# An LSTM on one core: the weight sums of the first steps made earlier in fixed rooms, and the projection's work dealt anew over steps 6 to 15

## The chip, the cores and the metric

One core of a Trainium2 chip. The metric is the device time of one run in microseconds, the median of the runs measured: 3111.43 us for the kernel before (3110.64 to 3113.64 in 3 runs).

## The reference

An LSTM of 512 units over 512 time steps, batch 32, with the input added to its output:

```python
xW = jnp.einsum('ntd,dg->ntg', x, Wx) + b
def step(carry, xw_t):
    a = xw_t + prev_h @ Wh
    i, f, o = sigmoid(a[:, :H]), sigmoid(a[:, H:2*H]), sigmoid(a[:, 2*H:3*H])
    g = jnp.tanh(a[:, 3*H:])
    next_c = f * prev_c + i * g
    next_h = o * jnp.tanh(next_c)
out = x + hs
```

x is 32 x 512 x 512, Wx and Wh are 512 x 2048, all in float32. Each step needs the h of the step before it, so the 512 steps come one after the other. The projection x @ Wx doesn't depend on h and can be made at any time ahead of its step.

## The kernel before

**The step.** For each t, h_part (L239, its matmuls are L248) multiplies the last h by Wh: 16 matmuls of 128 rows by 512 columns, four column tiles by four parts of the contraction, into one PSUM bank that already holds the projection of that step. cell (L252) follows on ScalarE (ACT: sigmoids and tanh, L263 to L270) and VectorE (DVE: products, sum and transposition, L267 to L274). GpSimd (POOL) adds x (L282), and SyncE's queue (SP) stores the output two steps at a time (L286). While the cell runs, TensorE (PE) has nothing of the recurrence to do, so the projection of later steps is put there.

**The projection.** Steps 20 to 499 are projected in 20 groups of 24 steps. A group is done by a scheme that multiplies sums of blocks of x (U) with sums of blocks of the weights (V) and puts sums of the products (W) together; U_SUMS and U_OF (L48), V_SUMS and V_OF (L55), W_SUMS and W_OF (L62) name the terms. A group has 20 *slots*, a slot has seven products, and a product is an *item*: four matmuls of 256 columns each (L522), or 4 *units* of 64 columns. So a slot has 28 units and a group 560. The sequence of items over all slots is *the stream*; emit_matmuls sends so many units of it. Around it stand:

- u_op (L427) on DVE, which makes the sum of x-blocks that a slot needs, 128 x 896, in one of six rooms of ubuf; pair_sum (L483 to L489) on DVE, four operations of 128 x 768 per group, which the U sums read.
- load_v (L601) on SP, which loads the V sums of a row of the stream from DRAM (vdram) into the ring vring of three places, 128 x 1792 for a full row. A place is free when the items of its old row are done.
- seed_banks (L552) on ACT, which copies a bias row into the PSUM bank of a slot whose products start from one. There are five such banks, xbank; a sixth, bbank, holds one product of each slot, two slots at a time.
- evacuate, which takes finished products out of the banks: copies on ACT (L568, L577, L584), sums on DVE (L578, L581, L574) into rooms of cbuf. A bank is free for the slot after the next ones only when these are done.
- w_op (L392) on DVE, 128 x 1024, which makes sums of products; when an output block is complete, SP stores it to DRAM (L408), and load_xw (L613) brings it back, a step at a time, three steps ahead.

**The order.** It is written by hand: each engine does its instructions in the order in which the Python emits them, and waits for what it needs. w_op and evacuation are sent by a running balance of DVE's time (room["dve"]). From step 16 on every step has a like share of the stream, 23 and a third units on average.

**The head.** Steps 0 to 19 are projected plainly (plain_block, L181): per step 32 matmuls of 256 columns. The plain blocks of steps 0 to 4 and 7 come before step 0; HEAD_PLAINS says which are done beside the cell of which step, and keep (L774) adds the bias to them, in place (L776), into xw (L779), or into a parking place in cbuf (L783), whence SP stores it to kept (L784). From step 6 to 15 HEAD_STREAM gives the units of the stream of each step, 560 together, the first group. AHEAD_OF_CELL says how many units are emitted between h_part and the cell of a step (24 where it says nothing).

**The weight sums.** In the head the V sums are made too, on DVE: V_DIRECT are single blocks, V_FIRST and V_STEPS name the slots that are made before step 0 and beside steps 0 to 4. v_add (L672) does a sum in three operations (or one, of two made sums), in a room of vroom: three places of vring and three pairs of ubuf's rooms, which both are free until the stream starts. v_store (L684) then writes it to vdram, a large and a small DMA on SP. The bias rows of the seeds are loaded (load_seeds L735, load_raw_seeds L749), reworked on DVE (early_seeds L739 and L743, late_seeds L754 to L757) and four of the six copied by one DMA of SP from cbuf to r1 (move_seeds, L761). early_seeds stands after the V sums of step 4, pair_sum and the first U sums in step 5, late_seeds in step 6, and move_seeds after the last plain block's keep, in step 7.

jobs is a table from step to a list of such DVE work; it is shared out behind the plain blocks of the step (L908 to L912).

Of the kernel before, what the change touches and what calls it, by code (L numbers as in the profile page):

```python
# [37 lines left out]
LATE = (454, 456, 458, 460, 462, 470, 471)  # L38

FIRST = 7  # L40
HEAD_PLAINS = ((14, 15), (6, 16), (5, 17), (18, 19), (8, 11), (12,), (13,), (9, 10))
HEAD_STREAM = (0, 0, 0, 0, 0, 0, 32, 32, 56, 60, 60, 64, 64, 64, 64, 64)
AHEAD_OF_CELL = {7: 16, 8: 12}
V_DIRECT = (0, 2, 6, 9, 18, 19)
V_FIRST = (1,)
V_STEPS = ((3, 4, 5), (7, 8, 10), (11, 12, 13), (14, 15), (16, 17))

U_SUMS = {6: {3: 1, 5: -1}, 7: {1: 1, 6: 1}, 8: {2: 1, 3: -1}, 9: {2: 1, 7: -1}, 10: {0: 1, 1: -1}, 11: {0: 1, 4: -1}}  # L48
U_OF = [
# [5 lines left out]
V_SUMS = {8: {0: 1, 4: 1}, 9: {3: 1, 7: 1}, 10: {5: 1, 8: -1}, 11: {6: 1, 8: -1}, 12: {6: 1, 9: 1}, 13: {5: 1, 9: -1}}  # L55
V_OF = [
# [4 lines left out]
]  # L61
# [39 lines left out]
def kernel(  # L101
# [18 lines left out]
    xbank = [psum.tile([P, W], F32, name=f"xbank_{i}") for i in range(5)]  # L120
# [29 lines left out]
    def xslot(c):  # L150
        return 2 if c in (2, NCHUNK - 1) else c % 2

    def load_x(c, a=0, b=TC):
        nc.sync.dma_start(
            out=xnat[:, xslot(c), a:b].rearrange("p t q b -> p (t q b)"), in_=x[c][:, a * P : b * P]
        )
# [71 lines left out]
    def bank_of(t):  # L228
        if t < 9:
            g0, g1 = gbank  # L230
            return [g0, g1, xbank[3], xbank[4], xbank[0], g1, g0, xbank[3], xbank[4]][t]
        return gbank[t % 2]

    def half_of(t, i):
# [60 lines left out]

    free_c = [*range(6), 8, 9, 10, 6, 7]
    last_x = []
    free_u = list(range(6))  # L300
    room = {"dve": 0.0}

    def take(pool):
# [330 lines left out]
    vroom = [vring[:, i] for i in range(3)] + [  # L634
        ubuf[:, 2 * i : 2 * i + 2].rearrange("p a b c -> p (a b c)").rearrange("p (k c) -> p k c", k=7) for i in range(3)
    ]
    free_v = list(range(6))
    vt = {}
    v_uses = {}
    for terms in [*V_SUMS.values(), *V_OF]:  # L640
        for i in terms:
            v_uses[i] = v_uses.get(i, 0) + 1

    def tail_sums(a, b):

        z, w = r1[:, a:b], r2[:, a:b]
# [17 lines left out]
    def v_add(terms):  # L664
        (a, sa), (b, sb) = sorted(terms.items(), key=lambda v: -v[1])
        op = add if sb > 0 else sub
        dst = free_v.pop(0)
        if a > 7 and b > 7:
            op(flat(vroom[dst]), flat(vroom[vt[a]]), flat(vroom[vt[b]]))
        else:  # L670
            for d, pa, pb in zip(split_parts(vroom[dst]), v_parts(a), v_parts(b)):
                op(d, pa, pb)  # L672
        for i in (a, b):
            v_used(i)
        return dst

    def v_used(i):
        if i > 7:
            v_uses[i] -= 1
            if v_uses[i] == 0:  # L680
                free_v.append(vt[i])

    def v_store(s, parts, whole=None):
        dma = lambda o, i: nc.sync.dma_start(out=o, in_=i)  # L684
# [17 lines left out]
    def v_sum(i):  # L702
        if i > 7 and i not in vt:
            for k in V_SUMS[i]:
                v_sum(k)
            vt[i] = v_add(V_SUMS[i])

    def v_slot(s):

        terms = V_OF[s]  # L710
        for i in terms:
            v_sum(i)
        if len(terms) > 1:
            d = v_add(terms)
            v_stores.append(lambda: v_store(s, split_parts(vroom[d]), vroom[d]))
            free_v.append(d)
        else:
            (i,) = terms
            parts = v_parts(i)
            v_stores.append(lambda: v_store(s, parts, vroom[vt[i]] if i > 7 else None))  # L720
            v_used(i)

    v_stores = []

    def flush_v():
        for f in v_stores:
            f()
        v_stores.clear()
# [30 lines left out]
    def move_seeds():  # L759
        whole = lambda t: t.rearrange("p a s c -> p (a s c)")  # L760
        nc.sync.dma_start(out=whole(r1[:, 6:8]), in_=whole(cbuf[:, 6:8]))  # L761
# [12 lines left out]
    def keep(p):  # L774
        if p not in SEEDED:
            add(bank_of(p), bank_of(p), bias_full)  # L776
            return
        if p < PARKED:
            add(xw[:, p % 3], park_bank(p), bias_full)  # L779
            return  # L780
        n = p - PARKED
        dst = parks[n % 6]
        add(dst, park_bank(p), bias_full)  # L783
        kept_stores.append(lambda: nc.sync.dma_start(out=kept[n], in_=dst))  # L784

    with tc.manual_schedule():
# [40 lines left out]
        flush_v()  # L827
        for t in range(KEPT):
            add(bank_of(t), bank_of(t), bias_full)
        keep(FIRST)  # L830
        jobs = {}
        for t, ss in enumerate(V_STEPS):
            jobs.setdefault(t, []).extend([lambda s=s: v_slot(s) for s in ss])
        jobs[4].append(early_seeds)
        jobs[5] = [lambda i=i: pair_sum(0, i) for i in range(4)] + [lambda: u_ahead(28)]
        jobs[6] = [late_seeds]
        dve_jobs = []

        HEAD_STEPS = STREAM0
# [10 lines left out]
        for t in range(T):  # L850
# [15 lines left out]
            if last_x and t == last_x[0] + 3:  # L866
                load_x(NCHUNK - 1)
            assert last_x or t < SPLIT - 4
            if t == 3:
                load_x(2, 4, 8)  # L870
                load_seeds(((4, 3), (5, 1)), nc.sync)
                load_group(0)
            if t == 4:
                load_raw_seeds()
            if PARKED <= t + 3 < HEAD + NG * GS:
                load_xw(t + 3)
# [1 line left out]
            if t < HEAD_STEPS:  # L878
                plain = [("plain", p) for p in (HEAD_PLAINS[t] if t < len(HEAD_PLAINS) else ())]
                n_plain += len(plain)  # L880
                left = HEAD_STREAM[t]
                chunks = []
                if t >= len(HEAD_PLAINS) - 1:
                    chunks.append(("stream", AHEAD_OF_CELL.get(t, 24)))
                    left -= chunks[0][1]
                while plain or left:
                    if plain:
                        chunks.append(plain.pop(0))
                    m = min(left, 12)
                    if m:  # L890
                        chunks.append(("stream", m))
                        left -= m
                assert t < HEAD_STEPS - 1 or sum(HEAD_STREAM) == R * 7 * 4
                todo = jobs.pop(t, [])
                plains = sum(k == "plain" for k, _ in chunks)
                for i, (kind, m) in enumerate(chunks):
                    if kind == "plain":
                        bank = park_bank(m) if m in SEEDED else bank_of(m)
                        room["dve"] = 3000.0
                        for cc in range(4):  # L900
                            plain_block(m, cc, bank)
                        if i == 0:
                            cell(t)
                            if t + 1 in SEEDED:
                                seed_step(t + 1)
                        keep(m)
                        if m == HEAD_PLAINS[-1][-1]:
                            move_seeds()  # L908
                        last = i == plains - 1
                        for _ in range(len(todo) if last else -(-len(todo) // (plains - i))):  # L910
                            todo.pop(0)()
                            flush_v()  # L912
                    else:
                        load_v_ahead()
                        u_ahead(m)
                        if i == 0:
                            room["dve"] = min(room["dve"], 1000.0) + PLAIN
                        evacuate()
                        if t >= HEAD_STEPS - 3 and dve_jobs:
                            dve_jobs.pop(0)()  # L920
                        u_ahead(m + 24)
                        while wqueue and (room["dve"] > 800 or len(free_c) < 3):
                            w_op()
                        seed_banks(m)
                        emit_matmuls(m)
                        room["dve"] += m * PROD / 4
                        if i == 0:
                            cell(t)
                            room["dve"] -= 2500.0
                            if t + 1 in SEEDED:  # L930
                                seed_step(t + 1)
                if t >= 4:
                    load_v_ahead()
                if t == 10:
                    assert not v_stores
                    load_group(1)
                    group_loaded = 2
                    dve_jobs += [lambda i=i: pair_sum(1, i) for i in range(4)]
                continue
# [34 lines left out]
            while due and plain_tail:  # L974
                p, c, q = plain_tail[0]
                m = 2 if due > 1 and q % 2 == 0 else 1
# [6 lines left out]
            for p in kept_late:  # L983
# [3 lines left out]
                dst = late_halves.pop(0).rearrange("p s c -> p (s c)")  # L987
# [54 lines left out]
```

## Time and profile before

| what | value |
|---|---|
| median of 3 runs | 3111.43 us (3110.64 to 3113.64) |
| the profiled execution | 3112.65 us, span 3110.9 us |
| mean granted clock of TensorE | 0.999 |
| TensorE busy in the span | 3092.5 us (99%) |
| VectorE, ScalarE, GpSimd busy | 2229.6, 1451.8, 232.3 us |
| moved by the DMA queues | 761.44 MB, mean 245 GB/s |

How to read the lines that follow: a line of a timeline has the start in us from the span's start, the duration, the engine, the line of the kernel, the operation, what it writes and reads with the shape, the count of records put together in it, and in brackets the idle time of the engine before it with what ended that. TensorE's ends are modelled and reach a little into the next record. A matmul of float32 leaves two records. On SP a line is an issue of DMAs, not their transport. A line of the table by stretches has the stretch, its length, and the busy time (and count) of each engine in it, the granted clock, the busy share of the DMA engines and what they moved.

### The profile page before, as it was taken

To read this page: it belongs to the slowest core of one execution; us is meant where nothing else is said; L and a number is where in the kernel's file an instruction comes from. 1 tells how busy PE (TensorE), PEld (TensorE's weight loads), DVE (VectorE), ACT (ScalarE), POOL (GpSimd) and SP (SyncE) were. 2 spreads that over 40 slices of the span, in tenths; PEclk is the share of its full clock that TensorE was granted. 3 is DMA by queue.
4 is the path that set the end of the run, shared out by engine and by line. 5 is a ranking of instruction groups with operands and counts; after the bars stand their busy time and mean duration, and the time that the engine had idled before them with its cause. 6 is when DMAs were issued, how large, how long until landed. Compare 5 with 4: busy or idle time off the path is not lost.

```text
span 3110.9 us, 109178 instructions
## 1 busy us (share of the span) xinstructions
PE 3092.5 (99%) x44064; PEld 1674.5 (54%) x44064; DVE 2229.6 (72%) x6217; ACT 1451.8 (47%) x5484; POOL 232.3 (7%) x508
## 2 busy tenths in 40 slices
PE   9999999999999999999999999999999999999999
PEld 6644555555555555555555555555555555555576
DVE  6677776767676767777676767677776767677644
ACT  1344444444444444444444444444444444444444
POOL 0000000000000000000000000000000000000010
PEclk9999999999999999999999999999999999999999
DMA  9787878787777778787877777787877777778630
GB/s 334 281 265 264 265 245 258 233 267 241 256 253 249 255 243 267 245 263 236 259 244 255 253 249 254 248 258 248 270 230 256 246 254 251 256 250 276 198 92 21
DMA packets 307705, 761.44 MB, mean 245 GB/s; under 512 B 49024, under 2 KB 91776, under 8 KB 306560
## 3 DMA queue, kind: packets, MB, share of 16 engines
q1 hardware_dynamic: 307200, 754.45, 74.3%
q8 instruction: 348, 5.70, 0.8%
q14 instruction: 157, 1.29, 0.1%
HBM read 573.90 MB, written 179.31 MB: 242 GB/s over the span
## 4 chain that ended last, share of the span: by engine, by line
PE 93%; DVE 1%; ACT 0%; issue 0%; ACTq 0%; DVEq 0%
PE gbank L248 53%; PE xbank L522 32%; PE bbank L522 5%; PE xbank L248 2%; PE xbank L190 1%; DVE cbuf L392 0%; DVE prod L267 0%; DVE s L268 0%; ACT s L263 0%; DVE hbuf L272 0%; ACT tanh_c L270 0%; DVE ht L274 0%; DVE cbuf L578 0%; ACT cbuf L584 0%; DVE ubuf L427 0%
## 5 line engine op out<-in xcount | busy, mean ns | idle before, releaser
L248 PE MATMUL gbank<-wh_sb,ht 128*32 128x512 f32 (+1 forms) x16224 | 1778.2, 576 | 2.0 <-DVE ht L274 1.1
L248 PEld LDWEIGHTS gbank<-wh_sb,ht 128*32 128x32 f32 x16224 | 611.3, 110 | 823.3 <-issue 703.9
L522 PE MATMUL xbank<-vring,ubuf 128*32 128x256 f32 (+1 forms) x15464 | 957.5, 365 | 6.3 <-DMA vring<-vdram 3.6
L263 ACT ACTIVATE s<-gbank 128x128 f32<-128x128 f32 x976 | 274.1, 281 | 1277.5 <-PE gbank L248 1277.0
L522 PEld LDWEIGHTS xbank<-vring,ubuf 128*32 128x32 f32 x15464 | 591.5, 110 | 366.0 <-issue 189.9
L267 DVE TENSOR_TENSOR prod<-s 128x128 f32<-128x128 f32 x1024 | 293.7, 287 | 625.3 <-ACT s L264 625.2
L392 DVE TENSOR_TENSOR cbuf<-cbuf 128x1024 f32<-128x1024 f32 x408 | 490.3, 1215 | 1.5
L282 POOL TENSOR_TENSOR oc<-xnat,ht 128x128 f32<-128x128 f32 x504 | 232.1, 461 | 2839.8 <-DVE ht L274 1452.6
L270 ACT ACTIVATE tanh_c<-s 128x64 f32<-128x64 f32 x1024 | 262.4, 256 | 246.5 <-DVE s L268 244.4
L274 DVE STREAM_TRANSPOSE ht<-hbuf 128x64 f32<-128x64 f32 x1022 | 250.8, 245 | 76.2 <-DVE hbuf L272 3.2
L630 ACT COPY gbank<-xw 128x512 f32<-128x512 f32 x463 | 278.8, 602 | 0.1
L268 DVE TENSOR_TENSOR s<-prod 128x64 f32<-128x64 f32 x1024 | 230.5, 225 | 35.2
L568 ACT COPY cbuf<-xbank 128x512 f32<-128x512 f32 x374 | 218.5, 584 | 43.4 <-PE xbank L522 22.2
L272 DVE TENSOR_TENSOR hbuf<-o,tanh_c 128x64 f32<-128x64 f32 x1024 | 212.6, 208 | 28.2 <-ACT tanh_c L270 27.9
L264 ACT ACTIVATE s<-gbank 128x64 f32<-128x64 f32 x976 | 226.1, 232 | 0.0
L578 DVE TENSOR_TENSOR cbuf<-xbank,cbuf 128x256 f32<-128x256 f32 x374 | 153.2, 410 | 77.4 <-ACT cbuf L577 74.6
L522 PE MATMUL bbank<-vring,ubuf 128*32 128x256 f32 (+1 forms) x2704 | 200.6, 355 | 1.9 <-DVE cbuf L574 1.9
L522 PE MATMUL xbank<-vring,xs 128*32 128x256 f32 (+1 forms) x2472 | 174.6, 374 | 1.6 <-ACT xbank L552 0.9
L522 PE MATMUL xbank<-vring,r 128*32 128x256 f32 (+1 forms) x2480 | 173.3, 372 | 0.0
L265 ACT ACTIVATE o<-gbank 128x128 f32<-128x128 f32 (+1 forms) x507 | 155.2, 306 | 0.0
L581 DVE TENSOR_TENSOR cbuf<-xbank,cbuf 128x256 f32<-128x256 f32 x374 | 151.9, 406 | 0.0
L574 DVE TENSOR_TENSOR cbuf<-bbank,cbuf 128x256 f32<-128x256 f32 x374 | 151.4, 405 | 0.0
(104 smaller groups left out, 1803.7 us busy)
## 6 DMA issues: line engine op xcount, KB each, us to landing
vring<-vdram SPq DMA_DIRECT2D x340, 896.0 KB, 5.6
xw<-xwd SPq DMA_DIRECT2D x1920, 64.0 KB, 4.5
xwd<-cbuf SPq DMA_DIRECT2D x221, 512.0 KB, 4.5
out_dram<-oc SPq DMA_DIRECT2D x255, 128.0 KB, 3.7
xnat<-in_x_dram SPq DMA_DIRECT2D x62, 512.0 KB, 5.3
xs<-in_x_grouped_dram SPq DMA_DIRECT2D x10, 1536.0 KB, 8.7
vring<-vdram SPq DMA_DIRECT2D x20, 768.0 KB, 6.6
r<-in_x_grouped_dram SPq DMA_DIRECT2D x10, 1536.0 KB, 8.8
```

What stands on the lines that cost most here:

```text
L248: nc.tensor.matmul(dst[j * B : (j + 1) * B], state["ht"][:, k], m, start=False, stop=True, skip_group_check=True)
L263: nc.scalar.activation(s[:, u, 0:2], g[:, n_, 0:2], AF.Sigmoid)
L264: nc.scalar.activation(s[:, u, 2], g[:, n_, 3], AF.Tanh)
L267: nc.vector.tensor_mul(prod[:, u], s[:, u, 0:2], s[:, u, 2:4])
L268: add(nxt[:, u, 3], prod[:, u, 0], prod[:, u, 1])
L270: nc.scalar.activation(tanh_c[:, HALVES[u]], nxt[:, u, 3], AF.Tanh)
L274: nc.vector.transpose(ht[:, 2 * u : 2 * u + 2].rearrange("p q b -> p (q b)"), hbuf[:, HALVES[u]])
L282: (nc.gpsimd if t < T - 8 else nc.vector).tensor_add(oc[:, tt % 2], x_of(t), ht)
L392: op(c_of(dst), c_of(src), c_of(bb))
L522: nc.tensor.matmul(dst[j * B : (j + 1) * B, cols], left_of(gr, s, r)[:, j * B : (j + 1) * B], vring[:, row % 3, RIGHT[r], cols], start=sta ...
L568: nc.scalar.copy(t[:, 0:4:3], xb.rearrange("p (n c) -> p n c", n=2))
L630: nc.scalar.copy(bank_of(t), src)
```

## The change

- **Rooms.** The list of free rooms of the V sums (free_v, v_uses, v_used) goes. V_ROOMS says for each sum in turn which of the six rooms it is put in; rooms 0 to 2 are vring's.
- **Times of the V sums.** Slot 3 (V_NEXT) is made among the bias adds before step 0, V_SUMS[8] in step 1, and V_STEPS has four entries in place of five, so the last slots, 15 to 17, are made in step 3. early_seeds stays in step 4, without V sums ahead of it.
- **Loads.** The second half of x's chunk 2 is loaded in step 9 (was step 3), the three raw bias rows in step 6 (was step 4).
- **Bias rows.** late_seeds and move_seeds go to step 8, behind its plain block; two rooms of cbuf (6 and 7), which these rows occupy, come into the list of free rooms then.
- **Plain blocks.** Block 10 stays in step 7 and block 9 goes to step 8 (both were in step 7); step 7's bank is gbank[1] (was xbank[3]). What is in jobs is shared out evenly behind the plain blocks.
- **Stream.** Steps 6 to 15 have 36, 36, 60, 60, 60, 60, 64, 60, 64, 60 units (were 32, 32, 56, 60, 60, 64, 64, 64, 64, 64), 560 as before. Ahead of the cell are 24 units in step 7 (were 16) and 4 in step 8 (were 12).
- **Second group.** Its x is loaded from step 8 (was 10) and its pair sums are made from step 10 (were from 13). load_v_ahead is called from step 3 at a step's end (was 4). ubuf's rooms are taken in the order 2, 3, 4, 5, 0, 1.

```diff
-HEAD_PLAINS = ((14, 15), (6, 16), (5, 17), (18, 19), (8, 11), (12,), (13,), (9, 10))
-HEAD_STREAM = (0, 0, 0, 0, 0, 0, 32, 32, 56, 60, 60, 64, 64, 64, 64, 64)
-AHEAD_OF_CELL = {7: 16, 8: 12}
+HEAD_PLAINS = ((14, 15), (6, 16), (5, 17), (18, 19), (8, 11), (12,), (13,), (10,), (9,))
+HEAD_STREAM = (0, 0, 0, 0, 0, 0, 36, 36, 60, 60, 60, 60, 64, 60, 64, 60)
+AHEAD_OF_CELL = {8: 4}
...
-V_STEPS = ((3, 4, 5), (7, 8, 10), (11, 12, 13), (14, 15), (16, 17))
+V_NEXT = (3,)
+V_STEPS = ((4, 5, 7), (8, 10), (11, 12, 13, 14), (15, 16, 17))
+V_ROOMS = (0, 1, 2, 3, 4, 5, 2, 1, 3, 0, 4, 5, 3, 2)
...
-            return [g0, g1, xbank[3], xbank[4], xbank[0], g1, g0, xbank[3], xbank[4]][t]
+            return [g0, g1, xbank[3], xbank[4], xbank[0], g1, g0, g1, xbank[4]][t]
...
-    free_c = [*range(6), 8, 9, 10, 6, 7]
+    free_c = [*range(6), 8, 9, 10]
-    free_u = list(range(6))
+    free_u = [2, 3, 4, 5, 0, 1]
...
-    free_v = list(range(6))
+    rooms = list(V_ROOMS)
...
-        dst = free_v.pop(0)
+        dst = rooms.pop(0)
...
         for t in range(KEPT):
             add(bank_of(t), bank_of(t), bias_full)
+            if t == 1:
+                for s in V_NEXT:
+                    v_slot(s)
+                flush_v()
...
-        jobs[4].append(early_seeds)
+        jobs[1].append(lambda: v_sum(8))
+        jobs[4] = [early_seeds]
         jobs[5] = [lambda i=i: pair_sum(0, i) for i in range(4)] + [lambda: u_ahead(28)]
-        jobs[6] = [late_seeds]
+        jobs[8] = [late_seeds, move_seeds, lambda: free_c.extend((6, 7))]
...
+            if t == 9:
+                load_x(2, 4, 8)
             if t == 3:
-                load_x(2, 4, 8)
                 load_seeds(((4, 3), (5, 1)), nc.sync)
                 load_group(0)
-            if t == 4:
+            if t == 6:
                 load_raw_seeds()
...
-                if t >= len(HEAD_PLAINS) - 1:
+                if t > 6:
                     chunks.append(("stream", AHEAD_OF_CELL.get(t, 24)))
...
-                        if m == HEAD_PLAINS[-1][-1]:
-                            move_seeds()
-                        last = i == plains - 1
-                        for _ in range(len(todo) if last else -(-len(todo) // (plains - i))):
+                        plains -= 1
+                        for _ in range(-(-len(todo) // (plains + 1))):
...
-                        if t >= HEAD_STEPS - 3 and dve_jobs:
+                        if t >= 10 and dve_jobs:
...
-                if t >= 4:
+                if t >= 3:
                     load_v_ahead()
-                if t == 10:
+                if t == 8:
                     load_group(1)
```

More of the change, by code (lines that the diff above doesn't have):

```diff
@@ L636 @@
     ]
-    free_v = list(range(6))
+    rooms = list(V_ROOMS)
     vt = {}
[L639 to L642, printed above, removed]
     def tail_sums(a, b):
@@ L672, in v_add @@
                 op(d, pa, pb)
-        for i in (a, b):
-            v_used(i)
-        return dst
[L677 to L681, printed above, removed]
+        return dst
     def v_store(s, parts, whole=None):
@@ L715, in v_slot @@
             v_stores.append(lambda: v_store(s, split_parts(vroom[d]), vroom[d]))
-            free_v.append(d)
         else:
@@ L720, in v_slot @@
             v_stores.append(lambda: v_store(s, parts, vroom[vt[i]] if i > 7 else None))
-            v_used(i)
     v_stores = []
```

## The prediction, made before the changed kernel was run

> **What bounds the kernel now.** I read the page first (sums, then the chain), then the table by stretches, then TensorE's timeline up to 210 us, and last the timelines of VectorE (DVE), ScalarE (ACT) and the DMA queue (SP) around TensorE's waits. The page:
>
> ```profile
> span 3110.9 us, 109178 instructions
> PE 3092.5 (99%) x44064; PEld 1674.5 (54%) x44064; DVE 2229.6 (72%) x6217; ACT 1451.8 (47%) x5484; POOL 232.3 (7%) x508
> PE 93%; DVE 1%; ACT 0%; issue 0%; ACTq 0%; DVEq 0%
> ```
>
> TensorE is busy 3092.5 of 3110.9 us, so only 18.4 us of the span can be won without taking matmuls away, and the order of matmuls in both kernels counts the same number. The table by stretches says where the 18.4 us lie:
>
> ```profile
> core 0: us, PE busy (x) PEld busy (x) DVE busy (x) ACT busy (x) POOL busy (x), PEclk, DMA share, GB/s
> 95.40:98.81 3.41, 1.39 (x24) 0.50 (x16) 3.17 (x13) 2.01 (x5) 0.46 (x1) 1.00 0.87 281
> 98.81:102.23 3.42, 3.20 (x32) 1.58 (x32) 1.98 (x3) 0.74 (x2) 0.00 (x0) 0.50 0.92 284
> 300.00:2900.00 2600.00, 2599.89 (x36100) 1370.10 (x36094) 1911.63 (x5332) 1258.84 (x4697) 200.62 (x437) 1.00 0.78 252
> ```
>
> From 300 to 2900 us 0.11 us are idle, and the change does not touch what follows. What it can move is the head, and there are eight waits of TensorE in it:
>
> ```profile
> 97.25 1.07 PE L522 MATMUL xbank<-vring,ubuf 128*32 128x256 f32 x16 [1.54 <-DMA vring<-vdram]
> 99.03 1.94 PE L522 MATMUL xbank<-vring,xs 128*32 128x256 f32 x16 [0.71 <-ACT cbuf L568]
> 103.78 1.07 PE L522 MATMUL xbank<-vring,ubuf 128*32 128x256 f32 x16 [1.26 <-DMA vring<-vdram]
> 155.77 1.07 PE L522 MATMUL xbank<-vring,xs 128*32 128x256 f32 x16 [0.90 <-ACT xbank L552]
> 159.76 0.64 PE L522 MATMUL xbank<-vring,ubuf 128*32 128x256 f32 x8 [0.77 <-DMA vring<-vdram]
> 167.71 1.93 PE L522 MATMUL xbank<-vring,ubuf 128*32 128x256 f32 x32 [1.28 <-ACT xbank L552]
> 180.56 0.64 PE L522 MATMUL xbank<-vring,ubuf 128*32 128x256 f32 x8 [1.45 <-DVE cbuf L578]
> 195.80 0.64 PE L522 MATMUL bbank<-vring,ubuf 128*32 128x256 f32 x8 [1.87 <-DVE cbuf L574]
> ```
>
> Their sum is 9.78 us. To it comes the clock: 98.81 to 102.23 ran at 0.50, so 3.42 us did 1.7 us of work. The head's losses are 9.8 + 1.7 = **11.5 us, the most that the change can win** (0.37%). A measurement of this kernel tells about 0.2%, 6.2 us, from no change.
>
> **The change, part by part.** Durations are rows of this execution (3112.65 us, span 3110.9, so 1.75 us lie around the span); I compare losses of the head and put the difference on the median, 3111.43, which is 1.2 us lower. Where something stands in the changed kernel comes from the two kernels' orders of instructions: I let each instruction begin when the one before it on its engine and the one it waits for are over. Laid out so, the old order gives 6.9 us for the waits on DVE and ACT whose rows sum to 5.5 (leaving out the first three and the DMA's 0.77), about a third of a microsecond too much each; I take that off below. Units first:
>
> ```profile
> 104.64 3.64 PE L248 MATMUL xbank<-wh_sb,ht 128*32 128x512 f32 x32
> 108.07 1.07 PE L522 MATMUL xbank<-vring,xs 128*32 128x256 f32 x16
> 109.80 3.71 PE L181 MATMUL gbank<-r,xnat 128*32 128x256 f32 x64
> 113.55 0.70 DVE L776 TENSOR_TENSOR gbank<-gbank,bias_full 128x512 f32<-128x512 f32 x1 [2.91 <-PE gbank L181]
> 114.16 0.41 DVE L578 TENSOR_TENSOR cbuf<-xbank,cbuf 128x256 f32<-128x256 f32 x1
> 115.15 1.08 DVE L427 TENSOR_TENSOR ubuf<-xs 128x896 f32<-128x896 f32 x1
> ```
>
> A recurrent part takes 108.07 - 104.64 = 3.43 us. Two items of the stream (8 units) lie between 103.78 and 104.64, so an item is 0.43 us. A plain block begun at 109.80 leaves TensorE free at 113.23 (64 records at the 0.054 us that follows from an item's 8 records in 0.43), and its bias add starts 0.32 us later. On DVE the add holds the engine 0.61 us (to the next start), and so on for each row.
>
> *Weight sums a step earlier, x and bias rows moved behind them.* In before the last weight sum is over at 83.3; in the changed order it stands in step 3, and the adds ahead of it end at about 75.6, 7.7 us earlier. Its stores are issued earlier, and the first three row loads with them:
>
> ```profile
> 85.12 3.71 SPq L684 DMA_DIRECT2D vdram<-vring x4
> 94.56 1.28 SPq L601 DMA_DIRECT2D vring<-vdram x3
> 118.29 0.53 SPq L761 DMA_DIRECT2D r<-cbuf x1
> 145.79 0.55 SPq L474 DMA_DIRECT2D r<-in_x_grouped_dram x1
> ```
>
> ```profile
> 82.08 1.28 DVE L672 TENSOR_TENSOR vring<-cbuf,vring 128x768 f32<-128x768 f32 x2
> ```
>
> ```profile
> DMA packets 3014, 5.15 MB, mean 368 GB/s; under 512 B 204, under 2 KB 826, under 8 KB 3011
> ```
>
> The second is the DMA view of 80 to 94 us: the engines moved 368 GB/s, near the 400 of the best stretch below, so of the 7.7 us only about 5 arrive: I put the first rows at 92 to 96 us instead of 97 to 104. The 1.54 and 1.26 us go. **What is late next** stands at the same place, on DVE and ACT:
>
> ```profile
> 88.87 0.69 DVE L779 TENSOR_TENSOR xw<-bbank,bias_full 128x512 f32<-128x512 f32 x1 [1.14 <-PE bbank L181]
> 89.48 0.95 DVE L483 TENSOR_TENSOR xs<-xs 128x768 f32<-128x768 f32 x1
> 95.21 0.28 DVE L267 TENSOR_TENSOR prod<-s 128x128 f32<-128x128 f32 x1
> 97.08 0.69 DVE L779 TENSOR_TENSOR xw<-xbank,bias_full 128x512 f32<-128x512 f32 x1
> 97.69 1.08 DVE L754 TENSOR_TENSOR cbuf<-cbuf 128x256 f32<-128x256 f32 x3
> 100.14 0.69 DVE L757 TENSOR_TENSOR cbuf<-cbuf 128x512 f32<-128x512 f32 x1
> 97.80 0.59 ACT L552 COPY xbank<-seeds_own 128x512 f32<-128x512 f32 x1 [0.76 <-DVE xw L779]
> ```
>
> The third item needs its bank seeded (L552), the seed needs the bank that the add at 97.08 reads, and that add stands behind 8.2 us of DVE work without a gap, begun by a plain block's end (the bracket at 88.87). None of it is moved. The seed is done at 98.39 in both. The idle time before 97.25 begins at 95.71, where the plain block's last matmul ends by the model; the next could begin some 0.25 earlier, at 95.45. With its rows there TensorE does two items (0.86) and waits from 96.3 to 98.4: **2.1 us** (was 1.54 + 0.71, with the 1.26 behind).
>
> *Bias rows' sums (late_seeds) from step 6 to step 8.* 97.69 to 100.83 is 3.1 us of DVE that lay beside TensorE's waits. At step 8 they stand behind plain block 9 and ahead of a U sum that the stream needs. DVE from TensorE's leaving the block: 0.32 + 0.61 (bias add) + 3.1 + 1.08 (L427) = 5.1 us. TensorE has seven items, 3.0 us: **2.1 us of wait**. If the sums were absent, 2.0 against 3.0, it would be 0: this is the edit's whole price.
>
> *Plain block 10 at step 7 with stream behind it.* DVE: 0.32 + 0.61 + 0.41 (L578) = 1.35 us to the release of the bank that the second item needs; one item is cover: **0.9 us**. In before a second plain block hid this.
>
> *Pair sums of group 1 from step 13 to step 10; steps 10 to 12 dealt 60, 60, 64.* Two sums of 0.87 us (a row like L483, to the next start) now come between evacuations and U sums. By the order three waits of 0.95, 0.45 and 1.3 us, less 0.4 for the bias of the layout: **2.3 us** (bounds 1 and 4; was 0.90 + 1.28).
>
> *Steps 13 and 15.* Before:
>
> ```profile
> 171.12 5.06 DVE L392 TENSOR_TENSOR cbuf<-cbuf 128x1024 f32<-128x1024 f32 x4
> 191.25 0.42 DVE L578 TENSOR_TENSOR cbuf<-xbank,cbuf 128x256 f32<-128x256 f32 x1 [0.68 <-ACT cbuf L577]
> 191.59 3.48 DVE L392 TENSOR_TENSOR cbuf<-cbuf 128x1024 f32<-128x1024 f32 x3
> 195.33 0.41 DVE L574 TENSOR_TENSOR cbuf<-bbank,cbuf 128x256 f32<-128x256 f32 x1
> ```
>
> At step 15 the chain from L578 to L574's end, 4.5 us, left 1.87 us of wait, so six items were beside it. The new deal leaves the same chain with four items: 1.87 + 2 x 0.43 = 2.7; I take **2.5**. At step 13 four output sums (5.06), two evacuations (0.7), a U sum (1.0), a cell (1.9, as from 95.21 to 97.08 above) and L574 (0.4) make 9.0 us ahead of a bank; a recurrent part and six items (6.0 us) cover it: 3.0, less the layout's third twice (DVE and ACT both stand in the chain), **2.4** (was 1.45). Bounds for both: 1.4 and 3.2 each.
>
> *DMA behind the moved loads.* No row shows the new order of the queue; I bound it by the two rates that the head's queue had:
>
> ```profile
> DMA packets 1103, 2.66 MB, mean 266 GB/s; under 512 B 116, under 2 KB 262, under 8 KB 1103
> DMA packets 730, 2.00 MB, mean 400 GB/s; under 512 B 85, under 2 KB 93, under 8 KB 729
> ```
>
> (94 to 104 us and 103 to 108 us. Sizes are those of the tiles: a full row 0.92 MB, a kept or bias row 0.26.) The fourth row load now has ahead of it the third row, two outputs, six kept stores and three bias rows: with it 4.3 MB from about 91 us, landing at 102 by the one rate and 107.3 by the other, and some latency behind; TensorE wants it at 106. From 0 to 3 us, I take 1.0. The seventh row stands behind move_seeds, which waits on SP for late_seeds (about 125 us): 0 to 0.6, I take 0.4. Then move_seeds (1.05 MB), three rows, group 1's x (1.57), half a chunk of x and an output block go ahead of the tenth, with it 7.1 MB from 125 us, landing at 143 to 152 where it is wanted at 146.5: 0 to 5, I take 1.5. Together **2.9 us** (0 to 8.6; was 0.77 and 1.26).
>
> *Clock.* The row of 95.40 to 98.81 holds 2.02 us of idle, and the next stretch of the same length ran at half; the 1.87 us at 195.80 was followed by full clock. The changed kernel has five waits of 2 us or a little more. How they fall is chance; I take one halved stretch, **1.7 us** (0 to 5).
>
> [...]
>
> Costed at nothing: rooms from a table (no instruction of its own); two weight sums moved up among the bias adds (the banks behind them are read by the cells of steps 2 to 4, with TensorE at plain blocks meanwhile; without that cover some 2 us each, a 0.95 and two 0.6 steps as at 82.08); the half chunk of x at step 9 (first read by POOL at step 20; without that time 256 KB, under 1 us at the rates below).
>
> **Sum** of the head's losses after: 2.1 + 2.1 + 0.9 + 2.3 + 2.5 + 2.4 + 2.9 + 1.7 = 16.9, against 11.5: **+5.4 us, 3116.8, called 3117**.
>
> **The rivals.**
> 1. *The loads come in a burst and the clock trips again and again.* For it: 7.1 MB behind one wait of SP, five waits near 2 us. Against: the queue had 400 GB/s when it was full. It decides from 300 GB/s down: 12.3 of engine waits + 6 of DMA + 3.4 to 5 of clock = 22.5, **3122.5**, slower than before by 0.35%.
> 2. *Rows in time, no half clock*: DVE's waits alone, 12.3 against 11.5, **3112**: no difference; the wait on DMA is replaced by one on DVE, exactly.
> 3. *The clock does not halve, DMA as forecast*: 15.2, **3115**.
> 4. *DVE is not the bound after step 9* (the other side): the waits at steps 13 and 15 are one backlog, which the lighter deal (60 for 64) drains; then rows in time and full clock leave 2.1 + 2.1 + 0.9 + 1 = 6.1 us against 11.5: **3106**. It decides where the output sums come in ones and twos, not in fours; the order of instructions has them in fours and threes, which speaks against it.
>
> **How the numbers follow.** Forecast (3115.5 to 3119) 0.39; rival 1 (3119 to 3125) 0.22; rival 2 (3110 to 3113) 0.14; rival 3 (3113 to 3115.5) 0.13; rival 4 (3102 to 3109) 0.12. Range for 8 in 10: 3108.5 to 3122.5; it leaves out most of rival 4 and the upper part of rival 1. Slower by over 0.2% is above 3117.65: rival 1 and four tenths of the forecast, 0.38. Faster is below 3105.2: half of rival 4, 0.06. Within: 0.56. The first three that lie within 0.2% differ in what the traces show, not in a verdict.
>
> **What would show it.** Right: the first wait of the stream named ACT L552 and 2 us long; a wait of about 2 us at step 8 on a U sum (L427's successor), with late_seeds ahead of it on DVE; L574 as releaser of the two last waits; DMA waits at the fourth and tenth row. Wrong: a first wait under 1 us, no wait at step 8, or any change of the stretch from 300 to 2900 us, which I hold equal.

## The result and the profile after

The changed kernel took 3119.07 us (median of 12 runs, 3116.80 to 3121.97), the kernel before 3112.23 in the 12 runs beside them (3110.55 to 3114.35): a ratio of 1.0022, 95% interval 1.0013 to 1.0031, or 6.8 us slower. The forecast was 5.4 slower (3116.8, called 3117). The profiled execution of the changed kernel took 3121.97 us, 2.9 more than its median; of before's, 3112.65. Line numbers differ: up to the weight sums they are higher by two (L524 is L522 of before, L554 is L552), behind them lower by thirteen (late_seeds is L741 to L744, move_seeds L748, the bias adds L763 and L766).

The page's sums and the table by stretches, after:

```profile
span 3120.1 us, 109177 instructions
PE 3097.1 (99%) x44064; PEld 1674.1 (54%) x44064; DVE 2232.1 (72%) x6217; ACT 1452.7 (47%) x5484; POOL 233.1 (7%) x508
```

```profile
300.00:2900.00 2600.00, 2599.79 (x36072) 1369.97 (x36068) 1913.84 (x5325) 1258.25 (x4690) 201.18 (x437) 1.00 0.78 252
```

From 300 to 2900 us nothing changed, 0.21 us idle against 0.11. All of it is in the head. TensorE's timeline after, its waits up to 210 us:

```profile
98.56 1.07 PE L524 MATMUL xbank<-vring,xs 128*32 128x256 f32 x16 [1.88 <-ACT xbank L554]
107.42 1.07 PE L524 MATMUL xbank<-vring,xs 128*32 128x256 f32 x16 [0.91 <-DMA vring<-vdram]
113.55 0.64 PE L524 MATMUL xbank<-vring,xs 128*32 128x256 f32 x8 [0.69 <-DVE cbuf L580]
127.14 1.93 PE L524 MATMUL xbank<-vring,ubuf 128*32 128x256 f32 x32 [1.88 <-issue]
136.52 4.05 PE L524 MATMUL xbank<-vring,ubuf 128*32 128x256 f32 x40 [2.71 <-DMA vring<-vdram]
154.46 1.07 PE L524 MATMUL xbank<-vring,ubuf 128*32 128x256 f32 x16 [0.53 <-ACT cbuf L586]
163.01 0.64 PE L524 MATMUL xbank<-vring,ubuf 128*32 128x256 f32 x8 [0.16 <-DVE cbuf L580]
165.91 1.07 PE L524 MATMUL xbank<-vring,ubuf 128*32 128x256 f32 x16 [1.17 <-ACT cbuf L586]
186.70 0.64 PE L524 MATMUL bbank<-vring,ubuf 128*32 128x256 f32 x8 [2.42 <-DVE cbuf L576]
203.40 0.64 PE L524 MATMUL bbank<-vring,ubuf 128*32 128x256 f32 x8 [2.31 <-DVE cbuf L576]
```

Their sum is 14.66 us, against 9.78 before. The two DMA waits ahead of 104 us are gone; the seed's wait is in their place (98.56), and four waits of about 2 us or more are new or larger. The clock adds to it. Stretches of 3.41 us of the changed kernel (length, busy time by engine, then the granted clock as the third number from the end), each wait followed by the stretch behind it:

```profile
133.17:136.58 3.41, 0.69 (x12) 0.10 (x8) 1.69 (x8) 1.36 (x7) 0.26 (x1) 1.00 1.01 415
136.58:140.00 3.42, 3.42 (x36) 2.12 (x40) 0.00 (x0) 0.59 (x1) 0.20 (x1) 0.50 1.01 401
184.37:187.79 3.42, 1.09 (x20) 0.68 (x24) 2.53 (x12) 2.06 (x6) 0.46 (x1) 1.00 1.00 288
187.79:191.20 3.41, 3.41 (x36) 1.74 (x32) 1.75 (x3) 1.07 (x3) 0.00 (x0) 0.50 0.98 380
201.44:204.86 3.42, 1.46 (x24) 0.76 (x28) 3.42 (x6) 0.32 (x1) 0.00 (x0) 1.00 0.26 99
204.86:208.27 3.41, 3.41 (x22) 1.08 (x16) 2.62 (x4) 0.05 (x1) 0.00 (x0) 0.50 1.01 253
95.62:99.03 3.41, 1.53 (x31) 0.85 (x26) 2.08 (x8) 2.10 (x5) 0.45 (x1) 1.00 1.03 392
99.03:102.44 3.41, 3.41 (x60) 1.81 (x56) 1.42 (x2) 1.98 (x4) 0.00 (x0) 1.00 0.63 204
```

Three stretches ran at 0.50 behind 2.72, 2.33 and 1.96 us of idle; behind 1.88 the clock stayed at 1.00. Three halved stretches are 3 x 1.7 = 5.1 us of work lost; before had one. Waits and clock make 14.66 + 5.1 = 19.8 us after and 11.5 before: 8.3 of the 9.3 us between the two profiled executions. The same sum, taken from the profiled execution's time, leaves 3100.2 to 3102.2 us in these two kernels and in every kernel below, so it accounts for each of them within about 1 us.

### The profile page after: what moved, and what is told of

Read it like the earlier page. It is cut to its first block, busy times and chain, and to the rows that moved or that the text cites. A ratio compares the mean times of both kernels' runs of the same rounds, so it can differ in the third digit from the quotient of the medians.

```text
span 3120.1 us, 109177 instructions
## 1 busy us (share of the span) xinstructions
PE 3097.1 (99%) x44064; PEld 1674.1 (54%) x44064; DVE 2232.1 (72%) x6217; ACT 1452.7 (47%) x5484; POOL 233.1 (7%) x508
## 4 chain that ended last, share of the span: by engine, by line
PE 97%; DVE 1%; DMA 1%; ACT 0%; SPq 0%; issue 0%; DVEq 0%; ACTq 0%
PE gbank L250 53%; PE xbank L524 33%; PE bbank L524 5%; PE xbank L250 2%; PE xbank L192 1%; PE xbank L183 1%; PE gbank L183 1%; DMA vring<-vdram 1%; DMA vdram<-vring 0%; DVE cbuf L394 0%; PE xbank L798 0%; PE bbank L183 0%; DVE prod L269 0%; DVE s L270 0%; SPq L771 0%
## 5 line engine op out<-in xcount | busy, mean ns | idle before, releaser
L524 PE MATMUL xbank<-vring,ubuf 128*32 128x256 f32 (+1 forms) x15464 | 961.1, 365 | 6.5 <-DMA vring<-vdram 2.7
L524 PEld LDWEIGHTS xbank<-vring,ubuf 128*32 128x32 f32 x15464 | 595.2, 110 | 365.4 <-issue 193.7
L524 PE MATMUL bbank<-vring,ubuf 128*32 128x256 f32 (+1 forms) x2704 | 200.8, 355 | 4.8 <-DVE cbuf L576 4.7
L524 PE MATMUL xbank<-vring,xs 128*32 128x256 f32 (+1 forms) x2472 | 174.1, 373 | 3.5 <-ACT xbank L554 1.9
L524 PE MATMUL xbank<-vring,r 128*32 128x256 f32 (+1 forms) x2480 | 173.8, 372 | 0.0
L576 DVE TENSOR_TENSOR cbuf<-bbank,cbuf 128x256 f32<-128x256 f32 x374 | 151.6, 405 | 0.1
```

The lines of the kernel that those rows point to most:

```text
L524: nc.tensor.matmul(dst[j * B : (j + 1) * B, cols], left_of(gr, s, r)[:, j * B : (j + 1) * B], vring[:, row % 3, RIGHT[r], cols], start=sta ...
```

## The experiments

All were timed in five rounds beside the kernel before; differences are to the median of before in the runs beside them (3113.10 in the first four, 3112.86 in the next four, 3112.46 in the last two). The intervals reach about 2.8 us to each side, so smaller differences between two experiments rest on their traces. The theory was that each part has its own price, set by the order on an engine; the rival, that the loads come in a burst and the DMA queue is the limit.

**1. The bias sums back in step 6.**

```diff
-            if t == 6:
+            if t == 4:
                 load_raw_seeds()
...
-        jobs[8] = [late_seeds, move_seeds, lambda: free_c.extend((6, 7))]
+        jobs[6] = [late_seeds]
+        jobs[8] = [move_seeds, lambda: free_c.extend((6, 7))]
```

> The changed kernel with the raw bias rows loaded in step 4 and their sums made in step 6 again, as before the change; move_seeds stays in step 8, all else as changed. Theory (the engines' orders): the 1.88 us wait at step 8 goes, because DVE has 3.1 us less ahead of the U sum; SP is no longer held until 126 us by move_seeds, so the seventh row load is issued some 3 us earlier and its 2.71 us wait shrinks to under 0.5; with it at least one halved stretch (1.7 us) goes. 4.5 to 6.5 us less than the changed kernel, 3113 to 3114.5. Rival (the burst of loads on the DMA queue): the loads still come together, the wait at the seventh or tenth row stays at 2 us or more, and only the 1.9 us go: 3117.

Measured 3113.53 us, +0.4 (ratio 0.9994 to 1.0012), where the changed kernel stood at +6.8. Both waits, at step 8 and at the seventh row, are gone, and with them one halved stretch (two were left). The wait of 0.91 us at the fourth row is gone, too: the raw bias rows are loaded in step 4 again, so the price of this part holds the moved load as well as the moved sums. The mechanism in the changed kernel, DVE's timeline:

```profile
122.28 0.70 DVE L763 TENSOR_TENSOR gbank<-gbank,bias_full 128x512 f32<-128x512 f32 x1 [1.61 <-PE gbank L183]
122.89 1.09 DVE L741 TENSOR_TENSOR cbuf<-cbuf 128x256 f32<-128x256 f32 x3
125.35 0.69 DVE L744 TENSOR_TENSOR cbuf<-cbuf 128x512 f32<-128x512 f32 x1
125.95 1.09 DVE L429 TENSOR_TENSOR ubuf<-xs 128x896 f32<-128x896 f32 x1
```

The U sum that TensorE needs begins when the bias sums end; it ends at 127.04, and the matmul that the timeline gives to "issue" begins at 127.14.

**2. The seventh row's load ahead of move_seeds.**

```diff
-        jobs[8] = [late_seeds, move_seeds, lambda: free_c.extend((6, 7))]
+        jobs[8] = [late_seeds, load_v_ahead, move_seeds, lambda: free_c.extend((6, 7))]
```

> The changed kernel with one call moved: the seventh row load is emitted ahead of move_seeds in step 8, so that it isn't held behind SP's wait for the bias rows' sums; all else as changed. Theory (SP's order): the load is issued at about 122 us, when its place in the ring is free, instead of 126.7; the 2.71 us wait goes and the halved stretch behind it with it; the wait at step 8 (1.9) stays. 2.7 to 4.4 us less than the changed kernel: 3114.7 to 3116.4. Rival (the queue's rate is the limit): the eighth or the tenth row is late in its place by 2 us or more, and the time stays within 1 us of the changed kernel's, 3118 to 3120.

Measured 3116.63 us, +3.5 (1.0002 to 1.0019): 3.3 less than the changed kernel, in the theory's range by the difference. SP's queue, changed kernel and experiment:

```profile
126.11 0.53 SPq L748 DMA_DIRECT2D r<-cbuf  x1
126.69 4.05 SPq L603 DMA_DIRECT2D vring<-vdram  x3
```

```profile
117.91 0.32 SPq L603 DMA_DIRECT2D vring<-vdram  x1
125.23 0.53 SPq L748 DMA_DIRECT2D r<-cbuf  x1
125.86 4.01 SPq L603 DMA_DIRECT2D vring<-vdram  x2
```

The load could have gone at 118 us; SP waited 8 us for the bias sums ahead of it. The rest of the burst is the same, and behind it only one wait of 0.29 us on a row was left (at the fourth row's place, ahead of it, 0.63 us stayed, which the timeline gives to ScalarE). So the place in SP's order made this wait; the amount of loads alone did not.

**3. One output sum behind each set of evacuations.**

```diff
-                        while wqueue and (room["dve"] > 800 or len(free_c) < 3):
-                            w_op()
+                        for _ in range(1):
+                            if wqueue and (room["dve"] > 800 or len(free_c) < 3):
+                                w_op()
```

> The changed kernel with at most one output sum (L394, w_op) behind each set of evacuations in steps 6 to 15, where it sends as many as the balance of DVE's time allows (up to four in a row); all else as changed. Theory (order on DVE): the waits of 2.42 and 2.31 us at steps 13 and 15 shrink to under 1 us each, and the two halved stretches that followed them go; waits up to 170 us stay as they are. 3 to 6.5 us less than the changed kernel, 3112.5 to 3116. Rival (DVE has too much to do in these steps, whatever the order): the sums that were put off pile up, the waits come a little later, and the time is that of the changed kernel within 1 us.

Measured 3112.49 us, -0.6 (0.9989 to 1.0007), 7.4 less than the changed kernel and more than the theory's 6.5. The waits of 2.42 and 2.31 are 0 and 0.65 us, and no stretch was halved, not even behind the seventh row, whose wait is still there (2.09 us, which the timeline gives to an instruction of DVE that was over by then):

```profile
134.96 2.37 PE L524 MATMUL xbank<-vring,ubuf 128*32 128x256 f32 x40 [2.09 <-DVE ht L276]
196.01 0.64 PE L524 MATMUL bbank<-vring,ubuf 128*32 128x256 f32 x8 [0.65 <-DVE cbuf L576]
```

**4. The early weight sums alone**, in the kernel before: V_NEXT, V_STEPS, V_ROOMS, the jobs of steps 1 and 4, free_u and the call of load_v_ahead as in the change, jobs[6], loads, blocks and deal as before.

> The kernel before with the first part of the change alone: the weight sums a step earlier in the rooms of the table, the U rooms in the new order, row loads from step 3 on; x, bias rows, plain blocks, stream and pair sums as before the change. Theory (the seed takes the place of the row loads): the three DMA waits at 97 to 104 us (1.54, the 0.71 behind it, 1.26) go and one wait of 1.9 to 2.2 us on the seed's copy (L554) comes; the rest of the head is as before. 1.3 us less by the waits; the halved stretch behind them may go or stay: 0 to 3 us less than before, 3109 to 3112. Rival (the row loads were the bound and nothing stands behind them): 3.5 us of waits and 1.7 of clock go, 3107.

Measured 3108.41 us, -4.7 (0.9977 to 0.9994). TensorE's first two waits:

```profile
98.75 1.07 PE L524 MATMUL xbank<-vring,xs 128*32 128x256 f32 x16 [1.88 <-ACT xbank L554]
152.49 1.07 PE L524 MATMUL xbank<-vring,xs 128*32 128x256 f32 x16 [0.90 <-ACT xbank L554]
```

The theory's mechanism: the seed stands where the rows stood, and the rest is as before. Waits are 8.14 us for 9.78, no halved stretch for one, 3.3 us by that count; the profiled executions differ by 3.8 and the medians by 4.7, more than the theory's 3. What the last microsecond is, wasn't found.

**5 and 6. Pair sums or deal?** Both on top of experiment 1:

```diff
-                        if t >= 10 and dve_jobs:
+                        if t >= HEAD_STEPS - 3 and dve_jobs:
```

> The kernel with the bias sums in step 6, and besides the second group's pair sums made from step 13 on again, as before the change; the new deal of the stream stays. Two theories for the waits at steps 13 and 15 (2.41 and 2.30 us in the kernel with the bias sums in step 6). The prediction's (the deal: fewer items lie beside the same chain): both waits stay, only the waits at steps 10 to 12 get about 1 us smaller, 3112 to 3113. The other (the pair sums: 3.5 us more of DVE in steps 10 and 11 put output sums off, which then stand four in a row in step 13): the wait at step 13 goes, with the halved stretch behind it, the one at step 15 stays, and those of steps 10 to 12 shrink by 1: 4 to 5 us less than with the bias sums in step 6 alone, 3108.5 to 3110.

```diff
-HEAD_STREAM = (0, 0, 0, 0, 0, 0, 36, 36, 60, 60, 60, 60, 64, 60, 64, 60)
+HEAD_STREAM = (0, 0, 0, 0, 0, 0, 36, 36, 56, 56, 56, 64, 64, 64, 64, 64)
```

> The kernel with the bias sums in step 6, and besides the stream dealt 36, 36, 56, 56, 56, 64, 64, 64, 64, 64, so steps 11 to 15 have 64 units as before the change; the pair sums stay at step 10. The prediction's theory (the deal): waits at steps 13 and 15 return to about 1.45 and 1.87 us and the two halved stretches go: 2 to 5 us less than with the bias sums in step 6 alone, 3109 to 3112. The other (the pair sums): DVE stays as late, the same losses show at other steps (a wait of over 2 us on a seed, L554, at step 11, and one of over 2 at step 13), and the time is the same or up to 4 us more, 3113 to 3117.

Pair sums at step 13: 3107.60 us, -5.3 (0.9975 to 0.9993), 5.7 less than experiment 1 and below the theory's range. The wait at step 13 is gone, those at steps 10 and 11 are 0.80 and 0.81 us (1.33 and 1.17 in experiment 1), and the one of 2.30 at step 15 stayed, this time without a halved stretch. Old deal (in steps 11 to 15; steps 6 to 10 have neither kernel's): 3116.62, +3.8 (1.0004 to 1.0022), 3.3 more than experiment 1. For step 13 the prediction's theory falls: with the pair sums late the new deal has no wait there, where the old deal has 1.45 us (experiment 4). DVE's timeline in the changed kernel, and with the pair sums at step 13:

```profile
152.41 0.95 DVE L487 TENSOR_TENSOR r<-r 128x768 f32<-128x768 f32 x1
154.27 0.95 DVE L489 TENSOR_TENSOR r<-r 128x768 f32<-128x768 f32 x1
158.41 0.95 DVE L491 TENSOR_TENSOR r<-r 128x768 f32<-128x768 f32 x1
178.21 5.00 DVE L394 TENSOR_TENSOR cbuf<-cbuf 128x1024 f32<-128x1024 f32 x4
```

```profile
157.91 3.68 DVE L394 TENSOR_TENSOR cbuf<-cbuf 128x1024 f32<-128x1024 f32 x3
165.64 2.47 DVE L394 TENSOR_TENSOR cbuf<-cbuf 128x1024 f32<-128x1024 f32 x2
169.38 1.22 DVE L394 TENSOR_TENSOR cbuf<-cbuf 128x1024 f32<-128x1024 f32 x1
170.85 0.95 DVE L485 TENSOR_TENSOR r<-r 128x768 f32<-128x768 f32 x1
```

With the pair sums late, six output sums are done between 157 and 171 us, where experiment 1 does three before its four in a row at 170.27 (at 178.21 in the changed kernel), ahead of the L576 that frees a bank. So the early pair sums push output sums back until four stand in a row; they aren't the only thing that can, since four stood in a row in the kernel before, too, with the old deal. In experiment 1 the first early pair sum also waited 1.69 us for its x; in the changed kernel it didn't, and the wait at step 13 is the same there (2.42, and 2.41), so this isn't its cause. What that load adds at step 10, no run parts from the sums.

The old deal with early pair sums gave a wait of 3.56 us at step 13, but there DVE stood idle ahead of the four sums, until the store of an output block had left cbuf:

```profile
173.04 5.07 DVE L394 TENSOR_TENSOR cbuf<-cbuf 128x1024 f32<-128x1024 f32 x4 [2.82 <-DMA xwd<-cbuf]
181.62 0.64 PE L524 MATMUL xbank<-vring,ubuf 128*32 128x256 f32 x8 [3.56 <-DVE cbuf L580]
```

So the 3.56 us can't be put to the pair sums alone, and experiment 6 doesn't say by itself what the deal costs at step 13. The wait of 2.30 at step 15 stayed with the pair sums at step 13, and one of 1.88 was there with the old deal: that part does belong to the deal.

**7. The seed in another bank**, on top of experiment 4:

```diff
-    park_banks = [xbank[1], xbank[2], bbank]
+    park_banks = [xbank[2], xbank[1], bbank]
```

> The kernel with the early weight sums alone, and besides the first two parking banks exchanged, so that plain block 13 is made in xbank[2] and not in the bank that the first seed needs. Theory (the seed waits for the bias add of block 13, 0.6 us, behind cell 6): the seed's copy starts some 0.8 us earlier, as soon as ACT has done the copy of step 7 (L632), and the wait of 1.88 us is 1.0 to 1.2: 0.7 to 0.9 us less than the early sums alone, 3107.5 against 3108.4 there. Rival (the wait's end is set by something else that ends at 98.5, a row of the ring or the tail of ACT's queue): no change.

Measured 3107.59 us, -5.3 (0.9976 to 0.9994); the wait on L554 is 1.03 us, at 97.40. The size is as expected, and it was the bias add of block 13 that the seed waited for; 0.8 us between medians of two rounds is itself at the edge of what the runs tell.

**8. Five edits on the changed kernel**: 1, 2, 3, 5 and 7 together.

> The changed kernel with five edits that the runs so far and the two beside this one bear on: bias rows and their sums in steps 4 and 6, the seventh row load ahead of move_seeds, the first two parking banks exchanged, one output sum behind each set of evacuations, pair sums from step 13. Theory: no wait over 1.3 us is left in the head and no halved stretch; waits of 1.1 at step 6, 0.7 at step 7, 1.0 at step 12 and under 3 together at steps 13 to 15 make 5 to 6 us against the 11.5 of before: 3106 to 3108, faster than both kernels and 1 to 2 us than the early sums alone. Rival (each wait taken away comes back at the next row load): 3110 or more.

Measured 3106.88 us, -6.0 (0.9974 to 0.9991), in the range; the waits are 1.03, 0.69, 0.79, 1.90, 0.54 and 0.19, so one of 1.90 was left where under 1.3 was expected.

**9. Pair sums back and nothing else**: the edit of 5 on the changed kernel.

> The changed kernel with the pair sums made from step 13 on again and nothing else undone. If the losses add up (theory: the pair sums' waits stand behind 150 us and the bias sums' ahead of it, each with its own halved stretches), it is as much less than the changed kernel as with the bias sums in step 6: 4.5 to 6 us, 3113 to 3114.5, with the waits at step 8 (1.9) and at the seventh row (2 to 2.7) still there and those at steps 12 and 13 gone. Rival (the same DVE backlog passes both places, so that with the bias sums at step 8 it only moves): 1 to 2 us less, 3117 to 3118.

Measured 3113.87 us, +1.4 (0.9993 to 1.0011), 5.4 less than the changed kernel (5.7 on top of experiment 1), in the theory's range. The losses add up. The seventh row's wait was 1.60 us, less than the 2 to 2.7 expected. Up to there SP's order of issues is that of the changed kernel (2.71) and of experiment 3 (2.09), so with one order this wait differed by 1.1 us between three profiled executions.

**10. The kernel before with four edits**: 3, 4, 7, and the stream dealt 32, 32, 60, 60, 64, 64, 64, 60, 64, 60.

> The kernel before with the early weight sums, the first two parking banks exchanged, one output sum behind each set of evacuations, and the stream dealt 32, 32, 60, 60, 64, 64, 64, 60, 64, 60. Theory (waits of the head add up): 1.0 at step 6, 1.3 to 1.8 on a seed at step 11, and under 2 together at steps 13 to 15, no halved stretch: 4 to 5 us against the 5.1 of the best kernel so far, 3105.5 to 3107, the same or up to 1 us less. Rival (the pair sums from step 13 need the heavy deal of steps 11 to 15 to stand beside): a wait of over 2 us there, 3108 or more.

Measured 3105.17 us, -7.3 (0.9965 to 0.9985), 0.25% faster than before and the fastest of all. TensorE's waits in the head, all five:

```profile
97.07 1.07 PE L524 MATMUL xbank<-vring,xs 128*32 128x256 f32 x16 [1.03 <-ACT xbank L554]
151.64 1.07 PE L524 MATMUL xbank<-vring,xs 128*32 128x256 f32 x16 [1.34 <-ACT xbank L554]
173.68 0.64 PE L524 MATMUL bbank<-vring,ubuf 128*32 128x256 f32 x8 [0.64 <-DVE cbuf L576]
177.45 0.64 PE L524 MATMUL bbank<-vring,ubuf 128*32 128x256 f32 x8 [0.55 <-DVE cbuf L576]
187.33 0.64 PE L524 MATMUL bbank<-vring,ubuf 128*32 128x256 f32 x8 [0.19 <-DVE cbuf L576]
```

3.75 us are left of 11.5. It keeps the first part of the change and leaves the others out; its deal is a third one.

## Why the prediction was right, and where it was not

| step of the prediction | forecast | measured | shown by |
|---|---|---|---|
| the seed takes the rows' place | 2.1 | 1.88 | 4, 7 |
| bias sums at step 8 | 2.1 | 1.88 | 1 |
| block 10 at step 7 | 0.9 | 0.69 | trace only |
| steps 10 to 12 | 2.3 | 0.53 + 0.16 + 1.17 | 5 |
| steps 13 and 15 | 2.4, 2.5 | 2.42, 2.31 | 3, 5, 6 |
| fourth, seventh, tenth row | 1.0, 0.4, 1.5 | 0.91, 2.71, 0 | 1, 2 |
| clock | 1.7 | 5.1 (profiled execution) | trace only |
| sum | 16.9 | 19.8 (profiled execution) | |

The time lay in the range, 2.1 us above the value and at the border between the forecast's band and rival 1's (3119); the difference to before was 6.8 us for 5.4. The mechanism was in the main the forecast one: rows earlier, then waits on DVE and ACT in their place. Of the signs that it named, the tenth row's wait alone did not come. The wait that the prediction and the experiments put at step 15 lies, by the recurrent parts' starts (191.86 and 204.89 us), at the end of step 14; its size, 2.31 for 1.87 before, is one item more (0.43 us), where the prediction counted two.

That the sum came so near is in part luck: the seventh row was 2.3 us above its term, the tenth 1.5 below, steps 10 to 12 0.4 below. Two steps failed, the seventh row and step 13, and for a third, the clock, the runs leave it open.

*The clock.* One halved stretch was taken, and three came in the profiled execution, 3.4 us more. It was the slowest of the 12 runs; how many stretches the others halved no profile tells. An estimate: the median run was 2.9 us faster, and with the same waits that leaves 5.1 - 2.9 = 2.2 us for its clock, near the term of 1.7. The waits then make 16.9 us with it, the forecast's sum, and about 1 us of the 6.8 lies outside of waits and clock (3102.2 is left, against 3101.2 before) and wasn't found.

*The seventh row.* 0.4 us was forecast, without a working. At the two rates that the prediction uses, 400 and 266 GB/s, move_seeds and the row (1.97 MB from 126.1 us) would have landed at 131.0 to 133.5 us, ahead of the 133.81 at which TensorE began to wait; the row landed at 136.4. The table by stretches of the changed kernel, from move_seeds' issue to the row's landing, and what its DMA view says of the loads of 126 to 140 us (KB each, median time to landing):

```profile
126.10:136.40 10.30, 6.66 (x88) 3.33 (x88) 7.84 (x18) 2.70 (x10) 0.07 (x1) 1.00 0.90 320
```

```profile
vring<-vdram SPq DMA_DIRECT2D x3, 896.0 KB, 10.2
```

The engines moved 320 GB/s for 10.3 us, 3.3 MB, where move_seeds and the row are 1.97: later loads moved beside it. In the kernel before, move_seeds and two rows behind it:

```profile
r<-cbuf SPq DMA_DIRECT2D x1, 1024.0 KB, 4.7
```

```profile
L601 SPq DMA_DIRECT2D vring<-vdram x2: 319/320/320, 123.4 to 126.5; - x2
DMA to landing us min/median/max: 4.6/4.7/4.7
```

There move_seeds, issued at 118.29, had landed before the first of the two rows went out, and the rows went 3 us apart, so little moved beside them.

*Step 13.* Its size was right (2.42 for 2.4), the cause wrong: the prediction put it to the deal of the stream and booked the pair sums at 2.3 - 2.18, next to nothing. Experiments 5 and 9 show that the pair sums cost 5.4 to 5.7 us, over half of it at step 13 and in the halved stretch behind it. The working counted what stands beside the chain, but not why four output sums stood in it.

By parts, from the medians: early weight sums -4.7, bias sums and their loads at step 8 +6.4 (6.8 - 0.4), pair sums at step 10 +5.7, and what is left, deal, blocks and x's loads, -0.6 (experiment 5 against 4), which is within the noise. They add to +6.8 by construction, each taken from the kernel before it in a row; the only price taken twice is that of the pair sums (5.4 in experiment 9). So the first part won nearly what it could, and two others lost it again more than twice over.

Rival 1 fits the time as well (3119 is its lower edge), and the clock of the profiled execution is as it says. But the burst as the cause of the waits falls: experiment 2 took the seventh row's away with the same burst behind it. Rivals 2 and 3 fall by the trace, with 3.62 us of waits on rows and three halved stretches. Rival 4 falls for the change as made, since the waits at steps 13 and 15 came; yet the lighter deal did drain step 13 once the pair sums were late again (experiment 5), and the wait at step 15 shrank to 0.65 us when the output sums were taken one by one (experiment 3).

## What to carry to other kernels

Before moving work earlier on an engine as busy as VectorE here (72%), lay out what it pushes back, and follow the pushed work to the next instruction that frees something another engine needs; the price shows there, about 25 us later here, and not at the place of the edit. Here move_seeds, a DMA that waited for VectorE, held the row load behind it on the same queue: the load was issued at 126.69 us, and at 117.91 where it stood ahead (experiment 2), so loads whose data are ready go ahead of it. With TensorE as the bound (busy 99%), nine of ten waits of 2.30 us or more (up to 3.56) cost 1.7 us beyond the timeline's bracket, by a halved stretch behind them, and eighteen of 1.86 to 1.91 us cost only themselves.

## What the runs showed of the hardware

In the 12 profiles (before, after and the ten experiments), of ten single waits of TensorE in the head of 2.30 us or more nine were followed by a halved stretch (3.41 us at a granted clock of 0.50), of eighteen from 1.86 to 1.91 none, and one of 2.09 was not. The tenth halved stretch, in the kernel before, came behind two waits (1.54 and 0.71 us), with 2.02 us of idle in the 3.41 us ahead of it.

In the changed kernel the halved stretches began at 136.58, 187.79 and 204.86: 51.21 and 17.07 us apart, 15 and 5 times 3.414. Counted off in such lengths from the halved stretches of the six profiles that have any, ten lengths in the head held 1.96 us of idle or more, and each was followed by a halved one; of those with 1.91 or less (1.91 in experiment 6) none was. The waits of 2.09 and 2.30 us that no halved stretch followed are in profiles without any to count from, so why the clock stayed there, no run shows.
